# An attention block and a depthwise convolution on one core: a column of taps on ScalarE, outputs on hardware queues, a shorter TensorE piece, and half of the last softmax division by way of DRAM

## The chip, the core and the metric

The kernel runs on one core of one Trainium2 chip. The metric is the device time of one execution in microseconds (us); less is better. The core has five engines that run their own instruction streams in order and meet through semaphores: TensorE (PE in the profile, with its weight loads as PEld), VectorE (DVE), ScalarE (ACT), GpSimd (POOL) and SyncE (SP). SP, ACT and POOL also issue DMAs, each in its own order.

## The reference

The input is x of 16 images, 384 channels, 32x32 pixels, all in fp32. Two layers follow each other:

```
# layer 0: attention over the 1024 pixels, 8 heads of 48 channels
xt   = tokens(groupnorm(x))                      # 32 groups of 12 channels
q, k, v = split(xt @ w_qkv.T)                    # per head
attn = softmax(q @ k.T * 48 ** -0.5)
x1   = x + (attn @ v) @ w_proj.T + b_proj
# layer 1: depthwise 7x7 convolution, padding 3
w_sym = mean of the four rotations of the 7x7 weight
out  = x1 + dwconv(groupnorm(x1), w_sym)
```

## The kernel before

**Tiles.** An image is three tiles of 128 channels x 1024 pixels. The eight heads make four pairs; a pair is a unit u, and an image has 4 of them (`NP`). A unit has two halves of 512 query pixels, and a half has 8 blocks of 128 key pixels (`NT`). The main loop (L1295) goes through the 16 images b in groups of 8 steps; r is the step number within the image, 0 to 56 by 8, so one group is one half of one pair, and r = 48 and r = 56 are the halves of the last pair.

**One group.** Eight score steps (`s_step`, L484): two matmuls into a PSUM tile, then `exp` on ScalarE. Then eight steps (`av_step`, L500) multiply by v. The accumulator has 64 rows for each head of the pair; row 48 of them is the sum of the exponentials, because v carries a column of ones. `take` (L514) copies the accumulator to `os_` on ScalarE.

**The division.** For every pair but the last of the last image, `finish` calls `sums_out` (L520): the sums' rows go to DRAM and come back as 128 partitions x 16 columns. `invert` (L529) takes reciprocals of that small tile, stores them to DRAM and reads them back broadcast to 64 partitions each; `divide` (L540) multiplies. These DMAs are all SP's. For the last pair of the last image, `divide_at_once` (L582) does a half in place: a TensorE matmul with a mask of ones spreads the sums over the partitions in PSUM, a VectorE reciprocal of 512 columns and a multiply follow. Its first half is called in the branch `ending` of the main loop (L1311), ahead of projections of the first two pairs; its second half in `fast_finish` (L1258), between projections of the third pair.

**The convolution.** A tile has 49 taps. On VectorE a tap is one `scalar_tensor_tensor` (`conv_tap`, L633): out += weight * shifted input, over the rows and columns that the shift leaves. The tiles of an image are worked in turn, one tap each (`tap`, L878, list `active`). VectorE does most of the convolution. Three tiles go to TensorE instead (`PE_TILES`, L140): (14,2), (15,2) and (15,1), named as (image, tile). For those, `conv_load` (L713) brings shifted copies of the normed tile from DRAM, on SP and, in the tail, also on ScalarE's queue. `conv_on_pe` (L735) multiplies them by small diagonal matrices, and it is cut into pieces of taps that are put between other work by `conv_piece` (L1232). `cuts` in `x1_chains` (L1080) sets the sizes of the pieces.

**Taps with dx = 0 for some tiles.** `ROWS_ONLY` (L143) lists tiles whose taps with no sideways shift, (dy, 0), are done elsewhere: ScalarE forms the product for a whole block of rows (`product`, L615), and a DMA of POOL adds it to the result in place (`add_rows`, L933). Tile (14,2) has three such rows (dy = 1, 2, 3), which `rows_early` (L937) does during image 15, through three scratch tiles that later hold image 15's normed input (`spare`). Tile (15,0), called `LONE`, has all seven, in a sum of its own (`sum3`); its other 42 taps alternate on VectorE between x1 and a second sum (`tap_of_two`, L899), and at the end L909 and L915 add the sums up.

**What sets the order.** A planner written in the kernel runs while the program is built. `clock` counts TensorE's planned time and `vclock` VectorE's. `after(wait, cost, f)` (L868) puts a step in a heap with a due time; `catch_up` (L954) fills VectorE's time up to TensorE's with steps that are due, and with taps otherwise, each at the price of `us_tap` (L874). ScalarE's extra work waits in `applies` with a due time and a cost, and `act_slot` (L1065) puts it where ScalarE is planned to have time. What is issued first in this plan stands first in each engine's stream.

**The end.** After the last projection the group statistics of image 15 are worked out on TensorE (`groups_on_pe`, L315: matmuls at L329), with convolution pieces between. Then xn1 of image 15 is formed, and the tail is the rest of tile (14,2), then (15,2) and (15,1) on TensorE, and what is left of image 14 and then (15,0) on VectorE. The outputs leave by `conv_end` (L646, POOL's queue), by L916 and by L774 for the two halves of (15,1), whose PSUM is added by VectorE (L773).

## Time and profile before

| | |
|---|---|
| time, median of 3 runs | 2911.26 us (2909.52, 2911.26, 2912.27) |
| the profiled execution's own time | 2910.11 us |
| its span, first to last instruction | 2908.2 us |
| granted TensorE clock | 0.998 |
| TensorE busy | 2896.8 us |
| VectorE busy | 2572.6 us, of which taps (L637) 2370.5 us |
| ScalarE busy | 1454.3 us, of which exponentials (L498) 952.4 us |
| POOL busy | 258.9 us |

The profile is of one execution, and its times count from the start of its span. In a row of the order of time, the first number is the start, the second the time from the first to the last of the instructions merged in it, then come the engine (SPq or POOLq: its queue of DMA issues), the line of the kernel, the operation, what it writes and reads, the shape, the count, and in brackets the idle time before it with what ended that. An fp32 matmul appears as two records. Records of TensorE overlap each other, so that a mean of 595 ns of one is no pace; the pace is read from the distance of their starts.

### The profile page before, as it was taken

The numbers are of one execution on the slowest core, as the hardware profiler recorded it, in microseconds if no ns is written. First come the engines' busy times: TensorE is split into PE (matmuls) and PEld (weight loads), VectorE is DVE, ScalarE is ACT, GpSimd is POOL, SyncE is SP. The second block draws the span as 40 slices with busy tenths as digits, with TensorE's granted clock in tenths as the row PEclk, the third lists the DMA queues.
The fourth block names the chain that finished last, engine by engine and source line by source line (L and its number), as shares of the span: only waits on it lengthen the run. The fifth ranks groups of instructions, "written<-read, shape, count | busy, mean of one in ns | idle before, by whom it ended". The sixth has DMA issues, their size and how long they took to land. (4 is left out here: it accounts for less than half of the span.)

```text
span 2908.2 us, 30141 instructions
## 1 busy us (share of the span) xinstructions
PE 2896.8 (100%) x11446; PEld 1174.4 (40%) x11446; DVE 2572.6 (88%) x2565; ACT 1454.3 (50%) x1738; POOL 258.9 (9%) x407
## 2 busy tenths in 40 slices
PE   9999999999999999999999999999999999999998
PEld 4343343433434343343433434343343433434333
DVE  5313999989899898998989899898998989899998
ACT  2545445465453645545465453645545455454531
POOL 3111004010100101000010100101001010100101
PEclk9999999999999999999999999999999999999999
DMA  7432012220312203022120212203012130212327
GB/s 285 132 28 63 16 36 77 37 68 20 66 35 43 70 21 84 16 35 70 35 71 16 64 41 43 69 23 84 16 36 70 29 77 16 61 44 43 90 70 181
DMA packets 73355, 172.84 MB, mean 59 GB/s; under 512 B 30432, under 2 KB 32368, under 8 KB 71664
## 3 DMA queue, kind: packets, MB, share of 16 engines
q0 software_dynamic: 33696, 112.73, 15.3%
q1 hardware_dynamic: 38080, 55.20, 7.8%
q10 hardware_dynamic: 1424, 2.88, 0.4%
q8 instruction: 92, 1.51, 0.2%
q14 instruction: 63, 0.52, 0.1%
HBM read 118.61 MB, written 28.72 MB: 51 GB/s over the span
## 5 line engine op out<-in xcount | busy, mean ns | idle before, releaser
L637 DVE SCALAR_TENSOR_TENSOR x<-xn,wsym,x 128x899 f32<-128x899 f32 (+9 forms) x2177 | 2370.5, 1163 | 136.0 <-ACT xn L361 136.0
L498 ACT ACTIVATE e<-ps_s 128x1024 f32<-128x1024 f32 x1024 | 952.4, 1051 | 54.4 <-PE ps_s L490 51.5
L490 PE MATMUL ps_s<-qk 48*128 48x512 f32 x4096 | 914.2, 596 | 1.1 <-ACT qk L446 1.1
L506 PE MATMUL acc<-e,v 128*64 128x512 f32 x4096 | 907.2, 595 | 0.0
L490 PEld LDWEIGHTS ps_s<-qk 48*128 48x128 f32 x4096 | 376.4, 185 | 535.1 <-ACT e L498 257.7
L506 PEld LDWEIGHTS acc<-e,v 128*64 128x64 f32 x4096 | 283.0, 137 | 608.2 <-issue 600.0
L439 PE MATMUL ps_qk<-x,wqk 128*128 128x512 f32 x1152 | 505.9, 595 | 0.0
L517 ACT COPY o<-acc 128x512 f32<-128x512 f32 x128 | 75.2, 587 | 607.6 <-PE acc L506 607.5
L439 PEld LDWEIGHTS ps_qk<-x,wqk 128*128 128x128 f32 x1152 | 216.4, 190 | 286.3 <-issue 285.9
L465 PE MATMUL ps_v<-wv,x 128*128 128x384 f32 x768 | 252.0, 488 | 0.0
L559 PE MATMUL ps_proj<-o,wp 128*128 128x512 f32 x540 | 234.2, 592 | 0.0
L446 ACT COPY qk<-ps_qk 128x1024 f32<-128x1024 f32 x96 | 96.7, 1009 | 253.1 <-PE ps_qk L439 253.1
L574 POOL DMA_DIRECT2D x<-in_x x45 | 39.4, 875 | 1802.1 <-ACT x L567 1424.2
L465 PEld LDWEIGHTS ps_v<-wv,x 128*128 128x128 f32 x768 | 144.6, 190 | 109.7 <-ACT e L498 12.1
L559 PEld LDWEIGHTS ps_proj<-o,wp 128*128 128x128 f32 x540 | 102.6, 190 | 125.9 <-issue 120.8
L474 ACT COPY v<-ps_v 128x384 f32<-128x384 f32 x128 | 55.1, 483 | 185.6 <-PE ps_v L465 185.6
L567 ACT ACTIVATE x<-ps_proj,bp 128x1024 f32<-128x1024 f32 x45 | 50.2, 1115 | 182.7 <-PE ps_proj L559 182.7
L542 DVE TENSOR_TENSOR o<-o,inv 128x1024 f32<-128x1024 f32 x63 | 76.9, 1221 | 70.1 <-DMA inv<-inv 65.2
L361 ACT ACTIVATE xn<-x,sc_x 128x1024 f32<-128x1024 f32 x47 | 54.9, 1231 | 76.3 <-DMA sc_x<-gr_x 65.5
L752 PE MATMUL ps_conv<-sh,mat 128*32 128x496 f32 (+3 forms) x656 | 67.9, 569 | 0.0
L384 DVE BATCH_NORM_STATS2 bs_all<-xs 128x6 f32<-128x512 f32 x84 | 52.1, 683 | 17.3 <-DMA xs<-in_x 17.2
L455 POOL DMA_DIRECT2D qk<-qk x96 | 47.4, 525 | 115.5 <-ACT qk L446 114.5
(142 smaller groups left out, 558.7 us busy)
## 6 DMA issues: line engine op xcount, KB each, us to landing
x<-in_x POOLq DMA_DIRECT2D x90, 512.0 KB, 5.6
inv<-inv SPq DMA_DIRECT2D x126, 256.0 KB
out<-x POOLq DMA_DIRECT2D x46, 512.0 KB, 4.0
xs<-in_x POOLq DMA_DIRECT2D x42, 512.0 KB, 6.3
qk<-qk POOLq DMA_DIRECT2D x96, 128.0 KB, 5.9
o<-o SPq DMA_DIRECT2D x90, 64.0 KB
sh<-xd SPq DMA_DIRECT2D x32, 160.0 KB
x<-in_x SPq DMA_DIRECT2D x6, 512.0 KB
```

The costliest lines, as they stand in the source:

```text
L439: nc.tensor.matmul(ps[:, h, :], lhsT=wqk[:, k, s, t, :], rhs=xns[b][:, k, h * HALF : (h + 1) * HALF], start=(k == 0), stop=(k == NK - 1),)
L446: nc.scalar.copy(halves(qks[u][:, s, :]), ps)
L465: nc.tensor.matmul(ps[:, j, 0:C], lhsT=xns[b][:, k, t * P : (t + 1) * P], rhs=wv[:, k, :], start=(k == 0), stop=(k == NK - 1),)
L474: nc.scalar.copy(dst.rearrange("p (h d) -> p h d", d=D + 1)[:, :, 0:D], ps[:, j, 0:C].rearrange("p (h d) -> p h d", d=D),)
L490: nc.tensor.matmul(ps[:, j, :], lhsT=qks[u][r, 1, i * P : (i + 1) * P], rhs=qks[u][r, 0, h * HALF : (h + 1) * HALF], start=True, stop=True,)
L498: nc.scalar.activation(es[n], ps, AF.Exp, scale=SCALE)
L506: nc.tensor.matmul(accs[u, h][64 * j : 64 * j + 64, :], lhsT=v_of(u, i, j), rhs=e[:, j, :], start=(i == 0), stop=(i == NT - 1),)
L517: nc.scalar.copy(os_[u][:, h * HALF : (h + 1) * HALF], accs.pop((u, h)))
L542: nc.vector.tensor_tensor(os_[u], os_[u], invs.pop(u), ALU.mult)
L559: nc.tensor.matmul(ps[:, h, :], lhsT=wp[:, t, o * P : (o + 1) * P], rhs=os_[NP * b + t][:, h * HALF : (h + 1) * HALF], start=(t == 0), sto ...
L637: nc.vector.scalar_tensor_tensor(acc, xn1s[b, k].rearrange("p (h w) -> p h w", w=W)[:, iy, ix], wsym[:, k, dy + PAD, dx + PAD : dx + PAD + 1],
L752: nc.tensor.matmul(dst[CH * i : CH * (i + 1), :].rearrange("p (y x) -> p y x", x=W)[:, :, ox], lhsT=mats[k][:, i, d0 * KS + dx + PAD, :], ...
```

## The change

There are five edits. (1) Tile (14,0), called `BESIDE`, joins `ROWS_ONLY` with all seven dy: it keeps 42 taps, ScalarE makes seven products during image 15, and POOL's DMAs gather six of them onto the seventh in `spare[15, 0]`; VectorE adds that tile once, behind the 42 taps. The list `early` holds these together with the three rows of (14,2), and they start at 2 us instead of 9 us, 7 us apart as before. Their products go through two scratch tiles instead of three. (2) The first half of the last pair is divided by way of DRAM (`half_sums`, `half_invert`, `half_divide`), begun behind the group r = 48; `divide_at_once` for that half and the planner's 4.2 us for it go. (3) Outputs of image 15 that POOL's queue issued are issued by ScalarE's. (4) The pieces of tile (14,2) are 5, 2, 2 and 4 taps of its first half instead of 7, 2, 2 and 2. (5) The planner prices a tap with 128 cycles of overhead even where only one tile is in turn.

```diff
             ROWS_ONLY = {PE_TILES[0]: (1, 2, 3), LONE: range(-PAD, PAD + 1)}
+
+            BESIDE = None if general else (B - 2, 0)
+            ROWS_ONLY[BESIDE] = range(-PAD, PAD + 1)
...
+            def half_sums(u):
+                sum_d = ddram.tile([2, HALF], F32, tag="sumh", name=f"sumh_{u}")
+                for j in range(2):
+                    r = 64 * j + D
+                    nc.sync.dma_start(sum_d[j : j + 1, :], os_[u][r : r + 1, 0:HALF])
+                late["sumh"] = small.tile([P, SC // 2], F32, tag="sumh", name=f"sumh_{u}")
+                nc.sync.dma_start(late["sumh"], sum_d.rearrange("j (p c) -> (j p) c", c=SC // 2))
+                after(7.0, 0.3, lambda: half_invert(u))
+
+            def half_invert(u):
+                nc.vector.reciprocal(late["sumh"], late["sumh"])
+                inv_d = ddram.tile([2, HALF], F32, tag="invh", name=f"invh_{u}")
+                nc.sync.dma_start(inv_d.rearrange("j (p c) -> (j p) c", c=SC // 2), late["sumh"])
+                inv = tpool.tile([P, N], F32, tag="t", name=f"invh_{u}")[:, 0:HALF]
+                for j in range(2):
+                    nc.sync.dma_start(
+                        inv[64 * j : 64 * j + 64, :], inv_d[j : j + 1, :].to_broadcast([64, HALF])
+                    )
+                after(9.0, 0.7, lambda: half_divide(u, inv))
+
+            def half_divide(u, inv):
+                half = os_[u][:, 0:HALF]
+                nc.vector.tensor_tensor(half, half, inv, ALU.mult)
+                late["half"] = True
...
             def conv_end(b, k):
-                nc.gpsimd.dma_start(
+
+                (nc.scalar if b == B - 1 and not general else nc.gpsimd).dma_start(
...
-                (nc.gpsimd, nc.sync)[h].dma_start(
+                (nc.scalar, nc.sync)[h].dma_start(
...
-                return ((H - abs(dy)) * (W - abs(dx)) + (128 if len(active) > 1 else 268)) / 955 + late_us
+                return ((H - abs(dy)) * (W - abs(dx)) + (128 if active else 268)) / 955 + late_us
...
                 taps = taps_of(b, k)
-                took = us_tap(*taps[n])
-                conv_tap(b, k, *taps[n])
                 c = active.pop(0)
                 c[2] += 1
-                if c[2] < len(taps):
+                if n < len(taps):
+                    took = us_tap(*taps[n])
+                    conv_tap(b, k, *taps[n])
+                else:
+                    assert not applies
+                    took = us_tap(0, 0)
+                    nc.vector.tensor_tensor(x1s[b, k], x1s[b, k], spare[B - 1, 0], ALU.add)
+                if c[2] < len(taps) + ((b, k) == BESIDE):
                     active.append(c)
...
             def add_rows(b, k, t, rows):
-                dst = late["sum3"] if (b, k) == LONE else x1s[b, k]
+                dst = {LONE: late.get("sum3"), BESIDE: spare.get((B - 1, 0))}.get((b, k))
+                dst = dst if dst is not None else x1s[b, k]
                 nc.gpsimd.dma_start(dst[:, rows], t, accum_op=ALU.add)
 
             def rows_early(b, k, n, dy):
-
-                t, rows = product(spare[B - 1, n % NK], b, k, dy)
+                if (b, k) == BESIDE and dy == 0:
+                    product(spare[B - 1, 0], b, k, dy)
+                    return
+
+                t, rows = product(spare[B - 1, 1 + n % 2], b, k, dy)
                 add_rows(b, k, t, rows)
...
-                        cuts = (0, KS, KS + 2, KS + 4) if b == B - 2 else (0, KS)
+                        cuts = (0, KS - 2, KS, KS + 2) if b == B - 2 else (0, KS)
...
-                    for n, dy in enumerate(ROWS_ONLY[PE_TILES[0]]):
+                    beside, first = BESIDE, PE_TILES[0]
+                    early = [(beside, 0), (beside, -1), (beside, 1), (first, 1), (beside, -2)]
+                    early += [(first, 2), (beside, 2), (first, 3), (beside, -3), (beside, 3)]
+                    for n, (bk, dy) in enumerate(early):
                         applies.append(
                             (
-                                clock + 9.0 + 7.0 * n,
+                                clock + 2.0 + 7.0 * n,
                                 1.3,
-                                lambda n=n, dy=dy: rows_early(*PE_TILES[0], n, dy),
+                                lambda n=n, bk=bk, dy=dy: rows_early(*bk, n, dy),
                             )
                         )
...
                 if ending:
                     catch_up(clock)
-                    divide_at_once(NP * b + NP - 1, 0)
-                    vclock += 4.2
                     for o in range(NK):
                         proj_part(b, o, (0, 1))
...
                 clock += (size * US_STEP + US_TURN) / 2
+                if b == B - 1 and r + 2 * size == PER_B:
+                    half_sums(n0 // (2 * NT))
                 if n0 // (2 * NT) < (n0 + size) // (2 * NT):
                     finish((n0 + size) // (2 * NT) - 1)
                 if ending:
                     catch_up(clock)
-                    assert not invs and not waiting
+                    assert not invs and not waiting and late["half"]
                     fast_finish(b)
```

## The prediction

> **What bounds the kernel now.** I read the page's busy shares first, then the chain that ended last, then stretches of the last image, then each engine's order of time there.
>
> ```profile
> PE 2896.8 (100%) x11446; PEld 1174.4 (40%) x11446; DVE 2572.6 (88%) x2565; ACT 1454.3 (50%) x1738; POOL 258.9 (9%) x407
> ```
>
> TensorE is busy for all but 11.4 us of the 2908.2 us span, so an edit can only shorten the kernel by removing TensorE work or by acting at the two ends. The busy times by stretch (us, then PE, PEld, DVE, ACT, POOL) say where those ends are:
>
> ```profile
> 2727.00:2798.00 71.00, 71.00 (x326) 25.89 (x322) 70.15 (x71) 42.57 (x49) 3.56 (x6) 1.00 0.39 106
> 2798.00:2841.00 43.00, 43.00 (x208) 17.91 (x208) 35.54 (x40) 5.59 (x11) 0.90 (x1) 1.00 0.06 16
> 2841.00:2902.00 61.00, 58.36 (x574) 25.18 (x562) 60.10 (x66) 11.24 (x11) 8.97 (x12) 1.00 0.82 207
> ```
>
> TensorE has no gap up to 2899.4. VectorE has 7.5 us of idle time between 2798 and 2841, and then none to its last instruction. The chain that ended last names VectorE alone, which is true only of the last two microseconds. Here is TensorE's order of time in the tail (start, us):
>
> ```profile
> 2828.31 5.90 PE L752 MATMUL ps_conv<-sh,mat 128*32 128x512 f32 x56
> 2834.14 1.72 PE L329 MATMUL ps_st_x<-mn_x,masks 128*128 128x1 f32 x14
> 2839.17 13.99 PE L752 MATMUL ps_conv<-sh,mat 128*32 128x496 f32 x136
> 2853.03 46.34 PE L752 MATMUL ps_conv<-sh,mat 128*32 128x512 f32 x445
> ```
>
> And VectorE's end:
>
> ```profile
> 2898.10 1.23 DVE L909 TENSOR_TENSOR sum<-sum,sum 128x1024 f32<-128x1024 f32 x1
> 2899.36 1.29 DVE L915 TENSOR_TENSOR x<-x,sum 128x512 f32<-128x512 f32 x2
> 2900.57 0.68 DVE L773 TENSOR_TENSOR x<-ps_conv,x 128x512 f32<-128x512 f32 x1
> ```
>
> TensorE ends at 2853.03 + 46.34 = 2899.37. The last VectorE instruction, which adds TensorE's last half tile, starts at 2900.57, 1.20 us after that. So two engines end nearly together, and **relieving VectorE alone is worth at most 1.2 us** before TensorE's end is the limit.
>
> **What the Trainium skill says.** (1) "DMA: Bandwidth & Descriptors", section "Anatomy of one DMA", gives about 2.0 us fixed for a DMA plus its bytes, and says that waits on semaphores are made by the issuing sequencer, not by the DMA engines. The page's fit is for POOL's software path. The trace is near it on SP's too: the read-back of the sums follows its write by 1.57 us (2777.95 to 2779.52). The second point it shows directly: POOL stands still for 8.49 us until an accumulate has landed:
>
> ```profile
> 2777.95 0.52 SPq L524 DMA_DIRECT2D sum<-o  x2
> 2779.52 0.34 SPq L525 DMA_DIRECT2D sums<-sum  x1
> 2787.70 0.34 SPq L533 DMA_DIRECT2D inv<-rec  x1
> 2789.12 1.09 SPq L536 DMA_DIRECT2D inv<-inv  x2
> 2790.45 9.76 SPq L718 DMA_DIRECT2D sh<-xd  x8
> ...
> 2878.20 0.56 POOL L647 DMA_DIRECT2D out<-x  x1 [8.49 <-DMA x<-conv]
> 2887.48 0.86 POOL L935 DMA_DIRECT2D sum<-tap_-3_13758  x1 [7.83 <-DMA sum<-tap]
> ```
>
> (2) "VectorE: DVE Perf Modes", section "Walkthrough: the 8-slice pipeline in each mode", says that Reciprocal is an iterative divide with a repeat count of 8. That agrees with 3.36 us for 512 columns below, against 0.69 us for a multiply of the same width.
>
> **The change, part by part.**
>
> Seven taps of tile (14,0) to ScalarE. VectorE loses 7 centre-column taps of 1024, 2x992, 2x960 and 2x928 elements. The rows of those widths in the tail are 1.23, 1.20 and 1.17 us long, but start 1.10 to 1.16 us after each other (2874.75, 2875.91, 2877.04, 2878.14), so I charge 7 x 1.12 = 7.8 us. It gains one whole-tile add, 1.23 us (L909). Net: 6.6 us of VectorE. ScalarE gains 7 products of some 1.1 us; the three that it has now (2.11 us for two) stand in the AV half of a step group, where ScalarE otherwise waits 3.7 to 5.5 us for the accumulator, so they are hidden. The queue of ScalarE work gives at most two products to a group of 14.08 us, since they fall due 7 us apart. Two scratch tiles replace three, so a product reuses one after 14 us; the three accumulates here took 4.3 to 5.5 us near this place and 8.4 at worst in the tail. POOL issues six more accumulates at some 0.9 us, while it would be idle from 2739 to 2839. Cost on the end: 0. Cost if that cover is gone: a stalled ScalarE delays the exponentials and TensorE with them, some 2 us for each late landing.
>
> First half of the last pair through DRAM. Removed: one TensorE matmul (L585, two records at 0.43 us apart: **0.86 us of TensorE, the only TensorE work that the change removes**), and VectorE's long reciprocal.
>
> ```profile
> 2799.61 3.36 DVE L587 RECIPROCAL inv<-ps_sum 128x512 f32<-128x512 f32 x1
> 2803.07 0.69 DVE L588 TENSOR_TENSOR o<-o,inv 128x512 f32<-128x512 f32 x1
> 2803.68 14.07 DVE L637 SCALAR_TENSOR_TENSOR x<-xn,wsym,x 128x900 f32<-128x900 f32 x13
> ...
> 2819.63 3.36 DVE L587 RECIPROCAL inv<-ps_sum 128x512 f32<-128x512 f32 x1 [1.87 <-PE ps_sum L585]
> ```
>
> Added: a reciprocal of 8 columns, about 0.25 us (L531 takes 0.23 to 0.26 for 16), and six SP DMAs. VectorE net: 3.1 us less. When does the inverse arrive? The accumulator's copy ends at 2792.0; the two row writes and the read-back follow to about 2794, landing near 2796 by the page's 2 us. The planner fires the small reciprocal where L587 is now, at 2799.6. SP is then still on the eight tap loads (2790.45 + 9.76 = 2800.2), the last four of which wait for the scores to release their buffer. So the inverse is stored at 2800.2. From store to broadcast took 1.42 us here and 5.06 us for the image's first pair (2723.12 to 2728.18); from broadcast to the multiply that waited for it, at most 5.0 us (2728.18 to 2733.21). Landing: 2806.6 to 2810.3. The multiply is planned 9 us after the reciprocal, at about 2809.5, behind taps. I take no stall; the late end is 0.8 us.
>
> What the planner does with the freed 4.2 us less the 1.0 charged: three more taps (3.2 us) ahead of the second half's reciprocal, so VectorE reaches that about as now, while TensorE's sum matmul arrives 0.86 us earlier. The 1.87 us of idle time there shrinks to about 0.9, so TensorE's path through it stays as it is.
>
> Short piece (5 taps instead of 7 ahead of the statistics). It moves 16 records, 16 x 0.103 = 1.65 us, from before the first average to after it. Averages start when the means are ready (a copy ending at 2832.48) instead of at 2834.14, so sc and the taps of image 15 come 0.86 + 1.65 = 2.5 us earlier. TensorE's total is unchanged; TensorE may now wait 0.1 to 0.2 us for the means. What is late next is TensorE itself.
>
> Hardware queues. Outputs of image 15 leave POOL for ScalarE's queue. The output of (15,2) waits there for its accumulate (7.10 us at POOL now); behind it on ScalarE are only two output issues, which no engine waits for. POOL's accumulates of sum3 no longer compete with those, but did not queue behind them before either. Cost and gain: 0, or up to 0.5 us at the last drain, as fewer transfers overlap there.
>
> Planner's dearer single tap (268 to 128 cycles, 0.15 us): reached when one tile is left. It can move a tap by one place; 0 to 0.15 us of VectorE per image, under TensorE.
>
> **The tail, summed.** VectorE after 2841.4 now does 30 + 21 taps:
>
> ```profile
> L637 DVE SCALAR_TENSOR_TENSOR x<-xn,wsym,x x30: 1076/1143/1233, 2841.4 to 2895.9; 128x899 f32<-128x899 f32 x7, 128x870 f32<-128x870 f32 x6, 128x841 f32<-128x841 f32 x4, 128x930 f32<-128x930 f32 x4
> L637 DVE SCALAR_TENSOR_TENSOR sum<-xn,wsym,sum x21: 1078/1139/1234, 2847.8 to 2896.9; 128x870 f32<-128x870 f32 x4, 128x899 f32<-128x899 f32 x4, 128x930 f32<-128x930 f32 x4, 128x841 f32<-128x841 f32 x2
> ```
>
> Tile (15,0) has 42 of them, so 9 are left over from image 14. Freed: 6.6 + 3.1 = 9.7 us, nine taps at 1.08. None is left over. VectorE then waits for xn of (15,0) until about 2841, and does 42 x 1.08 + 2.6 (checks and one L773) = 48 us, to 2889. The whole-tile add needs sum3: its five POOL accumulates shift 2.4 us with the statistics; the last, now issued at 2887.48 with 4.3 us to land, would land near 2890. Adds end near 2893, long before TensorE.
>
> TensorE ends at 2899.37 - 0.86 + 0.15 = 2898.66. Averages show that VectorE follows TensorE by 0.04 us (2835.86 to 2835.90), so the last L773 starts at 2898.7 instead of 2900.57: 1.87 us earlier. With 0.3 us for the drain, half of that bound and rounded: **2.2 us less**. The span becomes 2906.0 and the profiled execution 2910.11 - 2.2 = 2907.9. That execution is 1.15 us under the median of the three, so on the median: 2911.26 - 2.2 = **2909.1 us**. 0.2% is 5.8 us, about what a measurement can tell from no change.
>
> **Rivals.**
>
> A, the forecast: TensorE bounds the end; 2909.1, own range 2907.3 (stall at the second half gone, full drain gain) to 2910.8 (gain on TensorE eaten by the means and the landing). Chance 0.71.
>
> B, VectorE's end stays the bound: sum3's accumulates are pushed back on POOL, or taps are still left over. For: POOL waits 7 to 8 us for each landing, and add and output share its queue. Against: some 8 us of margin. With one landing (8.5 us) lost, the whole-tile add starts at 2898.5 and the last L773 2.47 us later, as now (2898.10 to 2900.57), at 2901.0: 0.4 us later than now, 2911.7. A second one lost would make it slow like C. Chance 0.12.
>
> C, slower: the inverse of the half comes late. VectorE stands at the multiply, the second half's reciprocal with it, and TensorE's last projection waits for both. Beyond 2810.4 (2809.5 and 0.9 of idle time) each microsecond is one of the span. At twice the measured worst, 20.2 us after the store, it lands at 2820.4: 10.0 late, less 2.2: 2919.1. Above 0.2% it decides from a landing at 2818.4. For: SP is in order and the loads use the same DMA engines. Against: 6.4 to 10.1 us in three rows here. Chance, with slips of ScalarE's cover at the same price, 0.13.
>
> D, faster by over 5.8 us: TensorE's end would have to move by 4 us, and only 0.86 us of its work goes. Chance 0.04.
>
> **How the numbers follow.** Faster 0.04 (D), same 0.71 + 0.12 = 0.83 (A, B), slower 0.13 (C). The range leaves out D and most of C: from 2906.5, A's low end less the 0.8 us by which the median stands above a low run here, to 2915, midway into C.
>
> **What would show it.** Right: TensorE gapless to about 2898.7, one L585 left, first L329 near 2831.8, no tap of image 14 after the statistics, the last L773 within 0.1 us of TensorE's end, VectorE idle 5 us or more in front of it. Wrong: a TensorE gap near 2822 with the multiply waiting for a DMA (C); the whole-tile add waiting for sum3 beyond 2898 (B); an exponential behind a product that waits for POOL.

## The result, and the profile after

| | before | after |
|---|---|---|
| median time | 2910.39 us (6 runs, 2908.08 to 2913.11) | 2922.58 us (6 runs, 2920.3 to 2925.59) |
| profiled execution | 2910.11 us | 2923.81 us |
| its span | 2908.2 us | 2921.7 us |
| granted TensorE clock | 0.998 | 0.995 |

The ratio is 1.0043 [1.0033, 1.0053]: 12.2 us slower, outside the predicted range of 2906.5 to 2915.0 us. In this section and the next, line numbers are those of the changed kernel, some 3 to 35 higher than before for the same code: L527 and L528 are `sums_out`, L598 and L600 `half_sums`, L604 to L609 `half_invert`, L616 `half_divide`, L588 to L591 the division in place of the second half, L625 `proj_part`, L666 a tap, L782 and L803 the convolution on TensorE and the add of its halves, L927 the whole-tile add of tile (14,0), L944 and L950 the adds of (15,0) at the end.

The busy times of the page, after:

```profile
PE 2900.7 (99%) x11444; PEld 1175.3 (40%) x11444; DVE 2562.9 (88%) x2559; ACT 1461.1 (50%) x1745; POOL 262.4 (9%) x411
```

TensorE has the two records less that the forecast names, yet is busy 3.9 us longer, and it is idle for 21.0 us instead of 11.4. VectorE is 9.7 us less busy, as worked out, and that bought nothing. Where TensorE stood shows in three stretches of its last projections (us, then PE, PEld, DVE, ACT, POOL, the granted clock, the DMA share and GB/s):

```profile
2810.00:2823.00 13.00, 13.00 (x47) 4.79 (x46) 3.09 (x3) 0.59 (x1) 0.00 (x0) 1.00 0.02 5
2823.00:2838.00 15.00, 3.03 (x5) 0.90 (x4) 12.64 (x11) 0.00 (x0) 0.70 (x2) 0.59 0.13 50
2838.00:2845.00 7.00, 7.00 (x14) 2.51 (x17) 4.89 (x6) 2.69 (x6) 0.00 (x0) 0.65 0.01 2
```

In the middle stretch TensorE works 3 us of 15. In the third it is busy all the time, at a clock of 0.65: **busy is not the same as fast**, and that is where the added busy time comes from. TensorE's order of time, after:

```profile
2819.11 1.02 PE L588 MATMUL ps_sum<-o,masks 128*128 128x512 f32 x2
2819.97 3.60 PE L625 MATMUL ps_proj<-o,wp 128*128 128x512 f32 x8
2825.93 2.07 PE L625 MATMUL ps_proj<-o,mat 128*128 128x512 f32 x2 [2.37 <-DVE o L616]
2837.60 7.15 PE L625 MATMUL ps_proj<-o,mat 128*128 128x512 f32 x10 [9.59 <-DVE o L591]
2844.68 4.32 PE L782 MATMUL ps_conv<-sh,mat 128*32 128x512 f32 x40
...
2869.39 45.87 PE L782 MATMUL ps_conv<-sh,mat 128*32 128x512 f32 x445
```

The brackets name both waits: first for the multiply of the first half (L616), then for that of the second (L591). VectorE's order of time shows that they are one wait:

```profile
2803.34 0.20 DVE L604 RECIPROCAL sumh<-sumh 128x8 f32<-128x8 f32 x1
2803.45 9.64 DVE L666 SCALAR_TENSOR_TENSOR x<-xn,wsym,x 128x841 f32<-128x841 f32 x9
2825.19 0.69 DVE L616 TENSOR_TENSOR o<-o,invh 128x512 f32<-128x512 f32 x1 [12.10 <-DMA invh<-invh]
2825.80 3.19 DVE L666 SCALAR_TENSOR_TENSOR x<-xn,wsym,x 128x900 f32<-128x900 f32 x3
2828.91 1.22 DVE L927 TENSOR_TENSOR x<-x,xn 128x1024 f32<-128x1024 f32 x1
2830.04 3.44 DVE L666 SCALAR_TENSOR_TENSOR x<-xn,wsym,x 128x841 f32<-128x841 f32 x3
2833.40 3.35 DVE L590 RECIPROCAL inv<-ps_sum 128x512 f32<-128x512 f32 x1
2836.85 0.69 DVE L591 TENSOR_TENSOR o<-o,inv 128x512 f32<-128x512 f32 x1
```

The small reciprocal is done at 2803.5. The multiply waits 12.1 us for the broadcast inverse, and six taps and the whole-tile add (7.6 us), then the long reciprocal, stand behind it in VectorE's stream. The sums of the second half were ready on TensorE's side at about 2820. The cause is in SP's order of DMA issues:

```profile
2793.44 0.53 SPq L598 DMA_DIRECT2D sumh<-o  x2
2794.94 0.35 SPq L600 DMA_DIRECT2D sumh<-sumh  x1
2795.38 0.38 SPq L536 DMA_DIRECT2D inv<-rec  x1
2796.86 1.10 SPq L539 DMA_DIRECT2D inv<-inv  x2
2798.17 3.91 SPq L748 DMA_DIRECT2D sh<-xd  x8
2818.02 0.53 SPq L527 DMA_DIRECT2D sum<-o  x2
2819.61 0.34 SPq L528 DMA_DIRECT2D sums<-sum  x1
2820.05 0.38 SPq L606 DMA_DIRECT2D invh<-sumh  x1
2821.50 1.09 SPq L609 DMA_DIRECT2D invh<-invh  x2
```

Between 2802.1 and 2818.0 SP issues nothing, although the store of the inverse (L606) has had its data since 2803.5. Ahead of it stand L527 and L528, the pair's ordinary `sums_out`. L527 needs the last accumulator, whose copy by ScalarE runs from 2817.40 for 0.59 us: it is issued 0.03 us after that copy ends, L528 1.59 us later, behind the write that it reads back, and the store 16.5 us after its data were ready.

**The planner explains the order.** `half_invert` falls due 7.0 us after the group r = 48. The next `catch_up` fills VectorE up to 7.04 us after it, in steps of about 1.1 us, so the step could fire there only if one of these ended within the last 0.04 us. It fires in the second `catch_up` of the branch `ending`, and `finish`, which issues `sums_out`, stands between the two. On VectorE that changes nothing, on SP it puts L527 ahead, as the rows above show.

The sum of the profiled execution, against before (first convolution record after the projections: 2844.68, before 2828.31). The waits are counted from the pace of the records (0.43 us, behind the first wait 0.86 us), and so come out a little longer than in the brackets. The twelve projection records before were:

```profile
2822.86 5.52 PE L596 MATMUL ps_proj<-o,mat 128*128 128x512 f32 x12
```

They start 2828.31 - 2822.86 = 5.45 us ahead of the convolution, of which 0.30 us is a wait.

| term | us |
|---|---|
| already late at 2640 us, before anything that the change touches | +1.39 |
| TensorE's sum matmul of the first half gone | -0.86 |
| TensorE waits: 2.53 for L616, 9.95 for L591, less 0.30 before | +12.18 |
| twelve projection records in 8.80 us (1.72 and 7.08) instead of 5.15 | +3.65 |
| convolution on TensorE, 70.58 instead of 71.06 us | -0.48 |
| last L803 starts 0.04 instead of 1.20 us after TensorE's end | -1.16 |
| from there to the end of the span, 6.40 instead of 7.63 us | -1.23 |
| outside the span, 2.11 instead of 1.91 us | +0.20 |
| sum (2923.81 - 2910.11 = 13.70) | +13.69 |

The first term is not the change's: up to there the two programs do the same, and the first new product of ScalarE starts at 2712.38 us. Most of it comes from the start of the execution: the first score matmuls start at 29.99 us instead of 28.85, 1.14 us later. After, TensorE's granted clock is 0.50 from 14 to 20 us; before, it is 0.57 from 14 to 18 us and full behind that. Such differences of the start come and go from one execution to the next, as the traces of the experiments show (below, with the last kernels).

The tail was as forecast, shifted as a whole. VectorE's end, after:

```profile
2903.48 1.08 DVE L666 SCALAR_TENSOR_TENSOR sum<-xn,wsym,sum 128x841 f32<-128x841 f32 x1
2908.85 1.23 DVE L944 TENSOR_TENSOR sum<-sum,sum 128x1024 f32<-128x1024 f32 x1 [4.29 <-DMA sum<-tap_-3_13783]
2910.11 1.30 DVE L950 TENSOR_TENSOR x<-x,sum 128x512 f32<-128x512 f32 x2
2911.32 0.68 DVE L803 TENSOR_TENSOR x<-ps_conv,x 128x512 f32<-128x512 f32 x1
2915.30 0.69 DVE L803 TENSOR_TENSOR x<-ps_conv,x 128x512 f32<-128x512 f32 x1 [3.30 <-PE ps_conv L782]
```

VectorE waits for sum3 and then for TensorE, and has 7.6 us of idle time in two gaps where it had none.

### The profile page after: what moved, and what is told of

Same layout as the page of the kernel before. It is cut to its first block, busy times and chain, and to the rows that moved or that the text cites. A ratio compares the mean times of both kernels' runs of the same rounds, so it can differ in the third digit from the quotient of the medians.

```text
span 2921.7 us, 30170 instructions
## 1 busy us (share of the span) xinstructions
PE 2900.7 (99%) x11444; PEld 1175.3 (40%) x11444; DVE 2562.9 (88%) x2559; ACT 1461.1 (50%) x1745; POOL 262.4 (9%) x411
## 4 chain that ended last, share of the span: by engine, by line
PE 99%; DVE 0%; DMA 0%; issue 0%; ACT 0%; SPq 0%; DVEq 0%
PE ps_s L493 31%; PE acc L509 31%; PE ps_qk L442 17%; PE ps_v L468 9%; PE ps_proj L562 8%; PE ps_conv L782 2%; PE ps_proj L625 1%; PE warm L1208 0%; PE ps_st_x L332 0%; DVE x L666 0%; DVE inv L590 0%; DMA invh<-invh 0%; DMA invh<-sumh 0%; DMA sum<-o 0%; DVE x L927 0%
## 5 line engine op out<-in xcount | busy, mean ns | idle before, releaser
L666 DVE SCALAR_TENSOR_TENSOR x<-xn,wsym,x 128x930 f32<-128x930 f32 (+9 forms) x2170 | 2364.1, 1172 | 139.1 <-ACT xn L364 138.9
L468 PEld LDWEIGHTS ps_v<-wv,x 128*128 128x128 f32 x768 | 144.6, 190 | 109.7 <-ACT e L501 12.1
L782 PE MATMUL ps_conv<-sh,mat 128*32 128x464 f32 (+3 forms) x656 | 67.4, 569 | 0.0
L534 DVE RECIPROCAL rec<-sums 128x16 f32<-128x16 f32 x63 | 16.1, 256 | 50.1 <-DMA sums<-sum 50.1
```

Of the source, the lines that this page charges most:

```text
L468: nc.tensor.matmul(ps[:, j, 0:C], lhsT=xns[b][:, k, t * P : (t + 1) * P], rhs=wv[:, k, :], start=(k == 0), stop=(k == NK - 1),)
L666: nc.vector.scalar_tensor_tensor(acc, xn1s[b, k].rearrange("p (h w) -> p h w", w=W)[:, iy, ix], wsym[:, k, dy + PAD, dx + PAD : dx + PAD + 1],
L782: nc.tensor.matmul(dst[CH * i : CH * (i + 1), :].rearrange("p (y x) -> p y x", x=W)[:, :, ox], lhsT=mats[k][:, i, d0 * KS + dx + PAD, :], ...
```

## The experiments

The ratio is to the kernel before on the same chip: 2910.25 us for the first four, 2910.21 for the next four and 2910.25 for the last four (medians of 25 to 34 runs). Every edit is to the changed kernel unless it says otherwise.

### The inverse by ScalarE's queue

```diff
-                nc.sync.dma_start(inv_d.rearrange("j (p c) -> (j p) c", c=SC // 2), late["sumh"])
+                nc.scalar.dma_start(inv_d.rearrange("j (p c) -> (j p) c", c=SC // 2), late["sumh"])
...
-                    nc.sync.dma_start(
+                    nc.scalar.dma_start(
```

> The store and the two broadcast reads of the half's inverse are issued by ScalarE instead of SyncE; nothing else. In ScalarE's order they stand right behind the copy of the last accumulator (which ended at 2818.0 us in the changed kernel's profile), no longer behind SyncE's write and read-back of the last pair's sums (store at 2820.05). Theory T, the place in the queue sets the landing and each microsecond of it is one of TensorE's: the store comes 2.0 us sooner, the multiply starts near 2823.2 instead of 2825.2, and the time falls by 2.0 us, to about 2920.6. Rival R1, the other four edits cost part of the 12 us: the same 2 us or less. Rival R2, the transfers by way of DRAM are slow in themselves: moving the store 2 us changes little, 2922 to 2923.

Measured: 2920.52 us, 1.0035 [1.0021, 1.0048]. ScalarE's order of time and VectorE's row (this run stands 0.08 us later there than the changed kernel's):

```profile
2817.48 0.59 ACT L520 COPY o<-acc 128x512 f32<-128x512 f32 x1 [16.02 <-PE acc L509]
2817.54 0.36 ACTq L606 DMA_DIRECT2D invh<-sumh  x1
```

```profile
2822.80 0.69 DVE L616 TENSOR_TENSOR o<-o,invh 128x512 f32<-128x512 f32 x1 [9.88 <-DMA invh<-invh]
```

Store, broadcast and multiply come 2.4 to 2.5 us earlier, and no more: on ScalarE the store stands behind the same accumulator's copy, of which SP only saw the end. Another queue with the same wait ahead of it is no way out; what was saved is SP's write and read-back of the sums (2818.02 to 2820.05) and little else.

### The sums behind the inverse

```diff
-                if n0 // (2 * NT) < (n0 + size) // (2 * NT):
+                if n0 // (2 * NT) < (n0 + size) // (2 * NT) and not ending:
                     finish((n0 + size) // (2 * NT) - 1)
                 if ending:
                     catch_up(clock)
+                    finish((n0 + size) // (2 * NT) - 1)
```

Only the order of issue changes. In this kernel and in the two built on it the kernel's own test of the sums' range reads the first half after its division, where its row holds ones. The outputs for this input do not depend on that, but a sum of this half that left the range would no longer be noticed. So the kernel shows the cause; the one without the read, further below, puts the true sums into the test.

> The write and read-back of the last pair's sums go behind the half's inverse in SyncE's order; everything else, VectorE's order included, is as in the changed kernel. Theory T: the store starts with the end of the small reciprocal, about 2803.6 us, the inverse lands near 2809, before VectorE reaches the multiply at about 2813; TensorE has no gap, and the time is the one of the forecast, about 2909 (0.9993 of the kernel before). Rival R1, the other edits cost some microseconds: 2912 to 2916. Rival R2, the way through DRAM is too slow in itself: the multiply still waits 5 us or more, 2916 or above.

Measured: 2907.50 us, 0.9992 [0.9983, 1.0000]. SP, then VectorE and TensorE:

```profile
2800.54 0.34 SPq L606 DMA_DIRECT2D invh<-sumh  x1
2804.82 1.09 SPq L609 DMA_DIRECT2D invh<-invh  x2
2815.74 0.53 SPq L527 DMA_DIRECT2D sum<-o  x2
```

```profile
2809.98 0.69 DVE L616 TENSOR_TENSOR o<-o,invh 128x512 f32<-128x512 f32 x1
...
2889.88 1.22 DVE L944 TENSOR_TENSOR sum<-sum,sum 128x1024 f32<-128x1024 f32 x1 [2.92 <-DMA sum<-tap_-3_13783]
...
2897.60 0.69 DVE L803 TENSOR_TENSOR x<-ps_conv,x 128x512 f32<-128x512 f32 x1 [4.57 <-PE ps_conv L782]
```

```profile
2822.37 4.56 PE L625 MATMUL ps_proj<-o,mat 128*128 128x512 f32 x10 [0.23 <-DVE o L591]
```

The multiply has no bracket: it waits for nothing. TensorE's ten records follow at full pace. These are the forecast's own pictures: multiply at about 2809.5, sum3 near 2890, last L803 0.1 us after TensorE's end (2897.52). With these DMAs behind the division, the whole loss is gone.

### The multiply behind the second half

The order on SP stays as in the changed kernel; the late inverse is allowed to be late.

```diff
-                after(9.0, 0.7, lambda: half_divide(u, inv))
+                late["half_step"] = lambda: half_divide(u, inv)
...
                 divide_at_once(NP * b + NP - 1, 1)
+                late["half_step"]()
```

> SyncE's order is as in the changed kernel, so the inverse lands as late as there (about 2824.9 us); but VectorE multiplies the first half behind the division of the second half instead of ahead of six taps, an add and the second reciprocal. Theory T: VectorE does its taps and the second half while the inverse is on its way; TensorE waits for the first half alone, from 2823.4 to about 2826, 2.6 us instead of 12 in all, and the time is about 2911.5. It says how much of the loss is the late landing and how much the work queued behind the waiting multiply: about 2.5 and 10 us. Rival R1: 2914 or above, since the other edits' cost stays. Rival R2 (only the landing counts, not what is queued behind): about 2922.

Measured: 2910.88 us, 1.0001 [0.9993, 1.0010]. VectorE, then TensorE:

```profile
2823.88 0.69 DVE L616 TENSOR_TENSOR o<-o,invh 128x512 f32<-128x512 f32 x1 [0.25 <-DMA invh<-invh]
```

```profile
2824.63 7.12 PE L625 MATMUL ps_proj<-o,mat 128*128 128x512 f32 x12 [2.90 <-DVE o L616]
```

The inverse is issued as late as ever (store at 2818.96), and the kernel loses 3.4 us against the repaired order instead of 15.1. So some 12 us of the loss are what was queued behind the waiting multiply, with part of the slow clock. The twelve records still take 7.04 us (to 2831.67) instead of 5.15: 1.9 us of half clock behind a gap of 2.9 us.

### The other four edits without the half

```diff
                     catch_up(clock)
+                    divide_at_once(NP * b + NP - 1, 0)
+                    vclock += 4.2
...
-                if b == B - 1 and r + 2 * size == PER_B:
-                    half_sums(n0 // (2 * NT))
```

> The changed kernel with the first half of the last pair divided in place again, as in the kernel before (mask matmul, reciprocal of 512 columns, 4.2 us in the planner); the other four edits stay. Theory T: they cost nothing; TensorE has its 0.86 us of sum matmul back, so about 2910 (0.9997 of the kernel before), with no tap of image 14 left in the tail and VectorE idle before the last add. Rival R1: some of the 12 us stays, 2913 to 2922. Rival R2 agrees with T here.

Measured: 2908.46 us, 0.9995 [0.9987, 1.0004]; the last L803 follows TensorE's end, 3.68 us after VectorE's other work. The other four edits show no cost. Set beside the repaired order (2907.5), the way through DRAM is worth at most about 1 us, which these runs do not tell from zero.

### The half alone, in the kernel before

`half_sums`, `half_invert`, `half_divide` and the call, put into the kernel before; nothing else.

```diff
-                    divide_at_once(NP * b + NP - 1, 0)
-                    vclock += 4.2
...
+                if b == B - 1 and r + 2 * size == PER_B:
+                    half_sums(n0 // (2 * NT))
```

> The kernel before with the half divided by way of DRAM and nothing else of the change. Theory T, the loss is this part's alone: VectorE stands some 12 us at the multiply, TensorE ends about 12.5 us later than before (near 2912 in the profile), VectorE, 12.1 us later and 3.1 us shorter, ends near 2910, so TensorE bounds the end: about 11.5 us more than the kernel before, near 2921.7. Rival, the loss needs the other edits too (more taps moved behind the wait, more transfers in flight): less than 8 us more, below 2918.

Measured: 2925.68 us, 1.0054 [1.0038, 1.0069]: some 4 us more than expected. VectorE, then TensorE (lines of this kernel: L612 is the half's multiply, L588 the second half's, L621 the projections):

```profile
2824.40 0.69 DVE L612 TENSOR_TENSOR o<-o,invh 128x512 f32<-128x512 f32 x1 [12.40 <-DMA invh<-invh]
2825.00 8.37 DVE L662 SCALAR_TENSOR_TENSOR x<-xn,wsym,x 128x900 f32<-128x900 f32 x8
```

```profile
2837.50 6.06 PE L621 MATMUL ps_proj<-o,mat 128*128 128x512 f32 x10 [11.23 <-DVE o L588]
```

The same stall with the same releaser: the part is enough by itself. Eight taps (8.4 us) instead of 7.6 us of work stand behind the multiply, and the ten records take 5.99 us where the pace of before gives 4.29, 1.7 us more; both were left out of the expectation. In this trace image 15 also begins 0.7 us later than before (its v matmuls at 2648.54 instead of 2647.85), and from the start of the last add to the end of the span it is 9.12 us instead of 7.63. Together these are 4.7 us, somewhat more than the 4 us that the expectation missed by.

### Due 5 us after the group instead of 7

```diff
-                after(7.0, 0.3, lambda: half_invert(u))
+                after(5.0, 0.3, lambda: half_invert(u))
```

> The changed kernel with one number changed: the small reciprocal falls due 5 us after the half's sums instead of 7, so that the planner takes it in the catch-up ahead of the projections. In VectorE's order the reciprocal moves up by one tap and one multiply and the half's multiply by two taps; in SyncE's order the store and the reads of the inverse now stand ahead of the last four tap loads and of the last pair's sums. Theory T: the multiply waits not at all or under 2 us, no gap of TensorE over 1 us: 2907 to 2909. Rival, the reads share the DMA engines with the tap loads and so still come late: the multiply waits 4 us or more, 2912 to 2916.

Measured: 2918.27 us, 1.0027 [1.0016, 1.0037]. **Neither expectation held.** SP, then VectorE:

```profile
2797.31 0.37 SPq L606 DMA_DIRECT2D invh<-sumh  x1
2801.53 1.09 SPq L609 DMA_DIRECT2D invh<-invh  x2
2802.72 1.94 SPq L748 DMA_DIRECT2D sh<-xd  x4
2815.26 0.53 SPq L527 DMA_DIRECT2D sum<-o  x2
```

```profile
2817.05 0.69 DVE L616 TENSOR_TENSOR o<-o,invh 128x512 f32<-128x512 f32 x1 [9.20 <-DMA sum<-o]
```

The store is now 18 us ahead of L527, and the multiply still waits, but what ends the wait is another DMA: the bracket names `sum<-o`, not `invh<-invh`. L527 reads the row of sums out of `o`, for both halves, and was issued earlier in the program than the multiply, which overwrites that row. So the multiply must wait for that read, and the read waits for the last accumulator. The theory of the queue's place alone was incomplete. There are **two locks with one key**, the last accumulator: the place on SP, and a write that must follow a read. The repaired order above opens both at once, so it could not tell them apart; the next two kernels do.

### Both locks, one at a time

The half's sums are read back once into their place among all the sums, and the pair's `sums_out` reads only the second half, so nothing reads what the multiply overwrites. In the first of the two kernels the step is due after 5.0, in the second after 7.0.

```diff
-                sum_d = ddram.tile([2, N], F32, tag="sum", name=f"sum_{u}")
+                n = HALF if u == U - 1 and not general else N
+                sum_d = ddram.tile([2, n], F32, tag="sum" if n == N else "sumh", name=f"sum_{u}")
+                c = SC * n // N
...
-                    nc.sync.dma_start(sum_d[j : j + 1, :], os_[u][r : r + 1, :])
-                nc.sync.dma_start(sums[:, u, :], sum_d.rearrange("j (p c) -> (j p) c", c=SC))
+                    nc.sync.dma_start(sum_d[j : j + 1, :], os_[u][r : r + 1, N - n :])
+                nc.sync.dma_start(sums[:, u, SC - c :], sum_d.rearrange("j (p c) -> (j p) c", c=c))
...
+                nc.sync.dma_start(
+                    sums[:, u, 0 : SC // 2], sum_d.rearrange("j (p c) -> (j p) c", c=SC // 2)
+                )
                 late["sumh"] = small.tile([P, SC // 2], F32, tag="sumh", name=f"sumh_{u}")
-                nc.sync.dma_start(late["sumh"], sum_d.rearrange("j (p c) -> (j p) c", c=SC // 2))
-                after(7.0, 0.3, lambda: half_invert(u))
+                after(5.0, 0.3, lambda: half_invert(u))
...
-                nc.vector.reciprocal(late["sumh"], late["sumh"])
+                nc.vector.reciprocal(late["sumh"], sums[:, u, 0 : SC // 2])
```

Due after 5.0:

> The due time of 5 us as in e6, and the last pair's sums are no longer read from the row that the half's multiply overwrites: the half's read-back lands in its place in the table of sums (the reciprocal goes to a tile of its own), and the last pair's write and read-back cover the second half alone. All sums reach the table. Theory T2, two locks hold the multiply, the inverse's place behind the last pair's sums on SyncE and the read of the row ahead of its overwriting: with both gone the multiply does not wait, TensorE has no gap over 1 us, 2907 to 2909. Rival, the inverse itself was late in e6 too (reads after the store took 4.2 us there): the multiply still waits 4 us or more, 2911 or above.

Due after 7.0:

> As e9, but with the due time of 7 us of the changed kernel: no read of the overwritten row any more, while the inverse stands behind the last pair's (now half as long) sums on SyncE. Theory T2: the queue's lock alone is enough, the inverse lands near 2824.5 in the profile and the time is the changed kernel's, 2921 to 2923. Rival, the overwritten row alone held the multiply: 2907 to 2909.

Measured: due after 5.0, 2908.35 us, 0.9994 [0.9985, 1.0002]; due after 7.0, 2923.10 us, 1.0043 [1.0029, 1.0057]. The multiply (L620 here) in the first and in the second:

```profile
2808.88 0.69 DVE L620 TENSOR_TENSOR o<-o,invh 128x512 f32<-128x512 f32 x1
```

```profile
2825.01 0.69 DVE L620 TENSOR_TENSOR o<-o,invh 128x512 f32<-128x512 f32 x1 [12.18 <-DMA invh<-invh]
```

With the read gone, 2 us of due time decide between no wait and 12.18 us. With the due time of 7.0 the queue alone makes the whole loss; with 5.0 and the read kept, the read alone makes 9.20 us of wait. Each lock is enough by itself.

### TensorE kept at work through the wait

```diff
+                warm = ps_o.tile([P, HALF], F32, tag="acc", name="warm_again")
+                for _ in range(15):
+                    nc.tensor.matmul(
+                        warm, lhsT=late["masks"][:, 7, :], rhs=os_[NP * b][:, 0:HALF], start=True, stop=True
+                    )
                 for o in range(NK):
                     proj_part(b, o, (NP - 1,))
```

This adds fifteen matmuls whose result nobody reads, to price the clock by itself.

> The changed kernel with 15 matmuls of 512 columns whose result nobody reads, on TensorE ahead of the last pair's projections, 15 x 0.86 = 12.9 us in the time in which TensorE waits for the divided halves. They add work and keep TensorE from standing still. Theory: in the changed kernel TensorE's granted clock falls to 0.50 in the wait, and the ten records behind it take 7.1 us instead of 4.3; without the standstill these 2.8 us come back: about 2919.8. Rival, the records are slow for another reason (operands, PSUM): no change, 2922 to 2923, or more by what the filler delays.

Measured: 2920.52 us, 1.0039 [1.0025, 1.0052]. TensorE:

```profile
2836.95 4.56 PE L625 MATMUL ps_proj<-o,mat 128*128 128x512 f32 x10 [0.24 <-DVE o L591]
```

The wait of VectorE is unchanged (12.48 us), but the ten records take 4.49 us instead of 7.08: 2.6 us in the trace, 2.1 in the medians, won by 30 records of useless work.

### What else the repaired kernels could gain

Two kernels give three taps of (15,1) from TensorE to VectorE (n counts VectorE's taps of tile (15,0)): one on the repaired order, one on the kernel without the read.

```diff
-                return [t for t in PE_TAPS if t != (1, 0) or (b, k) not in ROWS_ONLY]
+                given = {(1, 0)} if (b, k) in ROWS_ONLY else {(1, 3)} if (b, k) == PE_TILES[-1] else ()
+                return [t for t in PE_TAPS if t not in given]
...
+                if n in (10, 20, 30):
+                    conv_tap(*PE_TILES[-1], n // 10, 3)
```

> The repaired order (last pair's sums behind the half's inverse), and one TensorE tap of tile (15,1), which stands for three of the 49 (dy 1 to 3 at dx 3), is done by VectorE as three taps between those of (15,0). TensorE has 8 matmuls at 0.206 us less, 1.65 us; VectorE has 3 x 1.08 = 3.3 us more, less than its 2.9 + 4.6 us of waiting before the last adds. Theory T, TensorE alone bounds the end there: 1.6 us less than the repaired order, about 2905.9, and VectorE still waits for TensorE at the last add. Rival, VectorE or the accumulates on sum3 bound it: no gain, 2907.5 or above.

> e9 and the tap of tile (15,1) that e7 moved from TensorE to VectorE as three. Theory: the sum of both: e9's time less about 0.7 us, which is what e7 measured against e2, 2906 to 2907.5. Rival: no difference from e9.

Measured: 2906.73 us, 0.9993 [0.9984, 1.0001], and 2908.76 us, 0.9996 [0.9988, 1.0004]. The second equals the kernel it is built on (2908.35), the first is 0.8 us under its own. VectorE is not the bound in either: the last add starts right behind TensorE's end, at 2897.95 and 2899.09, after idle times of 3.65 and 1.53 us. The sixteen records less (445 to 429) shorten TensorE's last stretch by 0.6 us in the first trace (45.13 instead of 45.73) and by 1.9 in the second (44.15 instead of 46.06). The medians don't tell an expected 1.6 us from no change. In the second trace the gain was also lost again behind TensorE: ScalarE's queue issued the output of (15,2), which waits for an accumulate of POOL, at 2898.12 instead of 2893.71 us, and an output of (15,1) behind it at 2899.93 instead of 2894.73. From the start of the last add to the end of the span it is then 8.91 us instead of 6.37.

The last one takes edit 1 out of the repaired order: the seven taps of (14,0) go back to VectorE.

```diff
-            BESIDE = None if general else (B - 2, 0)
-            ROWS_ONLY[BESIDE] = range(-PAD, PAD + 1)
+            BESIDE = None
...
-                t, rows = product(spare[B - 1, 1 + n % 2], b, k, dy)
+                t, rows = product(spare[B - 1, n % NK], b, k, dy)
...
-                    early = [(beside, 0), (beside, -1), (beside, 1), (first, 1), (beside, -2)]
-                    early += [(first, 2), (beside, 2), (first, 3), (beside, -3), (beside, 3)]
+                    early = [(first, 1), (first, 2), (first, 3)]
...
-                                clock + 2.0 + 7.0 * n,
+                                clock + 9.0 + 7.0 * n,
```

> The repaired order without the first edit: tile (14,0) has its 49 taps on VectorE again, the three rows of (14,2) keep their former times. VectorE has 6.6 us more, some six taps of image 14 left over in the tail. Theory T, TensorE bounds the end, and VectorE's waits there (1.6 + 2.9 + 4.6 us in the repaired order) take the taps up: 2907.5 to 2908.5, that is, moving those taps to ScalarE bought at most 1 us. Rival, the taps are what made VectorE end in time: 2910 or above.

Measured: 2909.17 us, 0.9994 [0.9986, 1.0002], 0.7 us above the expected 2907.5 to 2908.5 and 1.7 above the repaired order, whose runs spread from 2905.7 to 2911.2. TensorE waits 1.42 us for the second half's division in this trace; whether the dearer VectorE stream causes it in every run was not tried.

No version beats the kernel before by more than a measurement tells: the best are 0.08 and 0.07% below it (0.9992 and 0.9993, with intervals that reach 1.0000 and 1.0001).

**The start moves every time by up to 2.7 us.** In the fourteen traces the mean clock of the first 40 us is 1.00, 0.96 or 0.91, and the first score matmuls start at 27.3 to 27.6, 28.6 to 29.0 or 29.7 to 30.0 us to match. None of the edits acts there. The kernel before has 0.96 in its trace, the change 0.91, the repaired order 1.00, the kernel without edit 1 again 0.91. Counted from the v matmuls of image 15 to the end of the span, where this is out of the way, a trace lasts 260.4 us before, 272.5 with the change, 257.0 in the repaired order, 257.4 without the read, 257.6 with the half in place and 258.0 without edit 1. By these the repaired kernels are some 2 to 3.5 us faster than before, the half is worth less than 1 us and edit 1 about 1 us; but each is a single trace, and the medians do not show it clear of noise.

## Why the prediction was wrong

**What bounds.** Right. VectorE lost 9.7 us of work and nothing came of it beyond its 1.2 us at the end: 1.16 of it shows in the sum above.

**Edit 1, ScalarE's products.** Right. Two products of 2.1 us stand in the AV half of a group (2744.85 to 2746.99), and the copy of the accumulator behind them still waits 3.58 us for TensorE. No exponential was delayed: each group's wait for its scores is 0.53 to 0.56 us, as before. In the repaired order no tap of image 14 was left over in the tail (from 2840.24 on, all are of tile (15,0)), and sum3 landed near 2890, as worked out.

**Edits 3, 4 and 5.** No cost showed: together with edit 1 they measured 0.9995 [0.9987, 1.0004]; none was run alone. From the start of the last add to the end of the span the traces with edit 3 have 6.2 to 6.9 us, with the one exception of 8.91, and the two without it 7.63 and 9.12, so the drain was worth some 1 us where 0.3 was taken. The exception shows what the forecast left out with "two output issues, which no engine waits for": no engine waits for them, but the end of the execution does. Edit 5 does nothing, against its description and the forecast's "268 to 128 cycles". `us_tap` now tests `active` instead of `len(active) > 1`, but `tap` calls it after it has taken the tile in turn off that list, where before it called it ahead of that. With one tile in turn the list is then empty, and the price is 268 as before.

**Edit 2, the half by way of DRAM: the step that failed** is "SP is then still on the eight tap loads (2790.45 + 9.76 = 2800.2) ... So the inverse is stored at 2800.2", and with it "Landing: 2806.6 to 2810.3" and "I take no stall". The tap loads were done by 2802.1 and held nothing up. The forecast had the planner fire the small reciprocal "where L587 is now", in the first `catch_up`; it fired in the second. The list of what the step is moved past was short by one entry: `sums_out` of the same pair, which `finish` puts on SP between the two calls of `catch_up`. The store went out at 2820.05 and the multiply ran at 2825.19. A second entry was missing in kind: the same DMA reads a row that the multiply overwrites. With both out of the way the forecast's numbers hold: store at 2800.54, multiply at 2809.98 without a wait, and 2.8 us less than before (2907.50 beside 2910.25; 1.9 in the kernel without the read; neither is clear of noise) where 2.2 was forecast.

**Rival C had the right place and the wrong cause.** It has VectorE stand at the multiply, "the second half's reciprocal with it, and TensorE's last projection waits for both", which is what the trace shows, together with the gap of TensorE that the forecast named as a sign of it; it put this down to slow transfers, and gave it a chance of 0.13. Its price rule works: the multiply at 2825.2, less the 1.4 us by which this run was late, is 13.4 us past its threshold of 2810.4, and 2911.26 + 13.4 - 2.2 = 2922.5 against a measured 2922.58. Part of that agreement is cancellation: against the rule the waits were 1.2 us shorter (12.18), the half clock cost 3.65 us that it does not have, and the gains were 3.5 us instead of 2.2.

**The clock was no term of the sum.** A wait of this length costs more than itself: the Trainium skill, "TensorE: Matmul & The Clock Gate", section "Part 1: The HAM clock gate", says that after about one idle window of 3.4 us TensorE runs at half rate until it has been busy for about as long. The trace agrees: ten records at 0.71 us instead of 0.43 behind the 9.95 us wait, and the kernel with TensorE kept at work has 2.6 us less. Where it differs stands in the last section.

**Where the gain was to come from.** Even with its order repaired, this part removes 0.86 us of TensorE and shows at most about 1 us. What it frees on VectorE is given to taps that TensorE's end does not wait for.

## What to carry to other kernels

Before a step is moved to a DMA queue, list everything that the program issues on that queue between its old and its new place, with what each entry waits for; one entry that waits for something late delays all behind it, ready or not, and another queue helps only if it has no such entry itself. For a step that overwrites, list the transfers that still read what it overwrites as well, because mending the queue alone uncovers them. An instruction whose input may be late goes behind the work that others wait for: here that order alone gave back some 12 of 15 us, with the input as late as ever.

## What the runs showed of the hardware

- **Half clock after less than one window.** In the kernel with the multiply behind the second half, TensorE was idle 2.90 us, and the clock granted from 2826 to 2828 was 0.50, with twelve records in 7.04 us. In the changed kernel the first gap, of 2.37 us, was enough: the clock from 2826 to 2828 was 0.50, and the two records behind the gap took 2.07 us. Gaps of 2.30 us (the half alone) and 2.04 (due after 7.0 without the read) were not enough: two records in 1.12 us. The skill's section puts a window at 3.4 us, and the same page's section "Why this matters for your kernels" names gaps above some 3 us as those to avoid; here shorter ones did it. The section calls the window free-running, which fits that nearly equal gaps differ, and how much the recovery differs: the ten records behind the long wait took 5.99 us (the half alone), 6.28 (ScalarE's queue), 6.94 (due after 7.0 without the read), 7.08 (the change) and 7.53 (due after 5), against 4.49 at full clock.
- **A small DMA behind loads in flight is slow.** The 4 KB store of the inverse let its broadcast go 1.45 us later on quiet DMA engines (2820.05 to 2821.50), and 4.28, 4.22 and 3.79 us later with tap loads of 160 KB in flight (2800.54 to 2804.82; 2797.31 to 2801.53; 2799.30 to 2803.09 without the read). Where the multiply then waited for nothing, it stood 9.4 us (repaired order) and 9.6 us (without the read) behind the store, so the landing lay inside the 6.4 to 10.1 us that the forecast took.
- **The clock of the start differs between executions.** With the same instructions up to there, it was 0.50 from 14 to 20 us in the change's trace and 1.00 in that of the repaired order, and the first score matmuls started at 29.99 and 27.40 us.
